# Attention and experts on one core: three buffers for the transposed tokens, loads one step further ahead, another order at the start

## The chip, the cores and the metric

The kernel runs on 1 core of a Trainium2 chip. The metric is the device time of one execution in microseconds; the time before is the median of 3 runs. The profile is of one further execution. TensorE (PE) multiplies matrices, VectorE (DVE), ScalarE (ACT) and GpSimd (POOL) work element by element, SyncE (SP) only issues transfers.

## The reference

The input is x, 8 batches of 512 tokens with 256 features, f32. What is computed, cut to what matters:

```python
xn = layernorm(x)
# attention: 16 heads of 64
q, k, v = split(xn @ qkv_w.T)
q, k = rope(q), rope(k)
scores = q @ k.T / 8 + (-p * log1p(a * abs(i - j)))   # p, a: one number per head
attn = softmax(scores) @ v
# experts: 16 of them, each token goes to its best one, at most 256 tokens each
gate = softmax(xn @ Wg); e = argmax(gate)
y = relu(xn_e @ w1[e]) @ w2[e] * gate[e]     # 0 for tokens beyond an expert's 256
out = x + attn @ out_w.T + y
```

## The kernel before

**Steps and stages.** The 16 heads are cut into 4 groups of 4. One step s is one group g = s // 8 with one batch b = s % 8, so there are 32 steps. A step has four stages dd = 0 to 3; d = 4 s + dd counts them through. A stage projects one of the four products that the next step needs (`project_qk(s + 1, pair, part)`: q or k of a pair of heads, 128 x 512), computes the scores of two units (`score`; a unit is one pair of heads and 128 queries, for which PE makes two 128 x 512 products, VectorE adds the bias and takes the row's bound, ScalarE takes exp), transposes the units of the stage before in 32 x 32 blocks on VectorE (`turn`), and, in every second stage, hands a pair's transposed scores to `move`. Attention times v (`attend`) follows five stages after; `project_out` for step s - 2 is in stage 0, `project_v` in stages 0 and 1.

**Queues.** The order on each engine is the order in which the program calls (`tc.manual_schedule()`): every engine works through its own list, and waits are on data and on buffers. SyncE's list holds nearly all transfers. `move` issues 16 transfers pt<-z of 128 KB, one rd<-turned and two rb<-rd (the reciprocal row sums, through HBM). Beside them stand the running sums y (`load_y`, `store_y`, 512 KB), the expert weights w, and xnT<-xnd.

**Transposed tokens.** `normalise(b)` makes the normalised tokens xn on ScalarE. `transpose_normed(b)` transposes them on PE, and ScalarE copies the result to the tile xnT (128 x 2 x 512). The first four batches use the pool `xpool` for it, with 2 buffers; the xnT of a batch is kept in HBM (xnd[b]) for the later groups. These stores, and those of xn (xrd), are put in the list `stores` and taken from it in later stages by POOL. From step 4 on, `load_normed(s)` loads the tile again: SyncE issues it at the end of stage 1 of step s - 2. With two buffers, the tile takes the place of that of step s - 2, whose last reader is `project_v(s - 2, 1)` in the same stage.

**The start.** Ahead of the loop, batch 0 is normalised and transposed, and the four products of step 0 are made: q and k of pair 0, then, after 14 matmuls whose result is not used (`keep_warm(14)`) and the scores of two units, q and k of pair 1. Each product is turned by its position (rope): VectorE swaps halves (`stream_shuffle` into sh), then three passes multiply by cos, by sin and add (`turn_by`). POOL makes the passes for all later products; at the start VectorE makes those of k of both pairs and of half of q of pair 0. `bias_tables` stage 1 scales the tables of the score bias on POOL.

**The middle and the end.** Up to step 3 the stages also hold the layer norm of the later batches and their logits (`moments`, `deviations`, `logits`), from stage 16 on the routing of the tokens to the experts (`route`, one piece a stage, on VectorE for the most part), and then the experts (`expert_work`), spread over the stages up to the last five steps. The experts' results are gathered and added in those last steps. The last step transposes its scores on PE (`turn_last`).

`product` makes each product of 128 output rows as two products of 64 rows, side by side in the array. It is line 200 of the profile for all projections and all products of the experts. PSUM pools: ps_sc (4 banks), ps_av (1), ps_mm (2), ps_po (1).

Of the kernel before, what the change touches and what calls it, by code (L numbers as in the profile page):

```python
# [19 lines left out]
P = 128  # L20
# [17 lines left out]
def attention_and_experts(  # L38
# [22 lines left out]
    rope = ctx.enter_context(tc.tile_pool(name="rope", bufs=2))  # L61
    xpool = ctx.enter_context(tc.tile_pool(name="xpool", bufs=2))
    ypool = ctx.enter_context(tc.tile_pool(name="ypool", bufs=2))
# [131 lines left out]

    def product(o, w, v, start, stop):

        for c in range(2):
            half = slice(c * D, (c + 1) * D)
            nc.tensor.matmul(o[half], w[:, half], v, start=start, stop=stop)  # L200


    mv = const.tile([P, NT, 2], F32, name="mv")
    rstd = const.tile([P, NT], F32, name="rstd")
    off = const.tile([P, NT], F32, name="off")

# [35 lines left out]

    def load_normed(s):
        xnT = xpool.tile([P, 2, S], F32, tag="xnT", name=f"xnT_{s}")
        nc.sync.dma_start(xnT, xnd[s % B])
        xnTs[s] = xnT
# [19 lines left out]
    def transpose_normed(b, copies=None):  # L266
        xn = xns.pop(b)
        if b < 4:
            xnT = xpool.tile([P, 2, S], F32, tag="xnT", name=f"xnT_{b}")
            xnTs[b] = xnT  # L270
        else:
            xnT = early.tile([P, 2, S], F32, tag="xt", name=f"xnT_{b}", bufs=2)
        for mc in range(2):
            pool, tag = ((ps_av, "av"), (ps_mm, "mm") if b == 2 else (ps_po, "po"))[mc]
            pt = pool.tile([P, S], F32, tag=tag, name=f"xt_{b}_{mc}")
            for i in range(TB):
                nc.tensor.transpose(
                    pt[:, i * P : (i + 1) * P], xn[:, i, mc * P : (mc + 1) * P], ident
                )
            (copies or (nc.scalar.copy,) * 2)[mc](xnT[:, mc, :], pt)  # L280
        stores.append(lambda: nc.gpsimd.dma_start(xnd[b], xnT))
        xns[b] = xnT
# [12 lines left out]
    def logits(b):  # L295

        xnT = xns.pop(b)
        pl = ps_po.tile([P, P], F32, tag="po", name=f"lgp_{b}")
        for mc in range(2):
            for i in range(TB):  # L300
                nc.tensor.matmul(
                    pl[i * 32 : (i + 1) * 32, :], wg[:, mc, :], xnT[:, mc, i * P : (i + 1) * P],
                    start=(mc == 0), stop=(mc == 1),
                )
        lgT[b] = early.tile([P, P], F32, tag="lgT", name=f"lgT_{b}")
        nc.scalar.copy(lgT[b], pl)
# [14 lines left out]
    def route():  # L321
# [30 lines left out]
        )  # L352
        slot = rp.tile([P, CAP], F32, name="slot")
        nc.gpsimd.iota(
# [31 lines left out]
        nc.vector.tensor_reduce(top, oh, AX.X, ALU.max)  # L386
        oh16 = rp.tile([P, NT, E], BF16, name="oh16")
        nc.vector.tensor_tensor(oh16, oh, spread(top), ALU.is_equal)
# [187 lines left out]

    def project_qk(s, pair, part, turn_too=True):
        g, b = divmod(s, B)
        wq, _ = weights[g]
        ps = ps_mm.tile([P, S], F32, tag="mm", name=f"qk_{s}_{pair}_{part}")  # L580
        c0 = part * GC + pair * P
        for mc in range(2):
            product(
                ps, wq[:, mc, c0 : c0 + P], xnTs[s][:, mc, :], start=(mc == 0), stop=(mc == 1),
            )
        sh = rope.tile([P, S], F32, tag="sh", name=f"sh_{s}_{pair}_{part}", bufs=3)
        nc.vector.stream_shuffle(sh, ps, ROT)  # L587
        t = qkpool.tile([P, S], F32, tag=f"qk{part}{pair}", name=f"t_{s}_{pair}_{part}")
        qk[s, pair, part] = t
        if not turn_too:  # L590
            return ps, sh, t
        nc.scalar.copy(t, ps)  # L592
        turn_by(nc.gpsimd, t, t, sh, slice(0, S))
# [6 lines left out]
    def project_v(s, i2):  # L600
        g, b = divmod(s, B)
        wq, _ = weights[g]
        if i2 == 0:
            vals[s] = qkpool.tile([P, TB, GC], F32, tag="v", name=f"v_{s}")
        pool, tag = ((ps_av, "av"), (ps_mm, "mm"))[i2]
        ps = pool.tile([P, 2, GC], F32, tag=tag, name=f"v_{s}_{i2}")
        for i in range(2):
            c0 = (2 * i2 + i) * P
            for mc in range(2):
                product(  # L610
                    ps[:, i, :], xnTs[s][:, mc, c0 : c0 + P], wq[:, mc, 2 * GC :],
                    start=(mc == 0), stop=(mc == 1),
                )
        nc.scalar.copy(vals[s][:, 2 * i2 : 2 * i2 + 2, :], ps)
# [166 lines left out]

    def project_out(s, i2, o=None):
        o = o or oTs
        _, wot = weights[s // B]
        ps = ps_mm.tile([P, 2, DM], F32, tag="mm", name=f"po_{s}_{i2}")
        for i in range(2):
            c0 = (2 * i2 + i) * P
            for pair in range(2):
                product(
                    ps[:, i, :], o[pair][:, c0 : c0 + P], wot[:, pair, :],  # L790
                    start=(pair == 0), stop=(pair == 1),
                )
# [62 lines left out]
    keep_warm(8)  # L855
    rotation(1)
    nc.vector.tensor_scalar_max(ab[:, 1, :], ab[:, 1, :], 0.01)
    bias_tables(0, 0, 1)
    moments(1, (0,))
    transpose_normed(0, (nc.vector.tensor_copy, nc.vector.tensor_copy))  # L860
    moments(1, (1,))
    deviations(1, 2, nc.gpsimd)
    q0 = project_qk(0, 0, 0, False)
    k0 = project_qk(0, 0, 1, False)
    nc.scalar.copy(q0[2][:, 2 * P :], q0[0][:, 2 * P :])
    normalise(1)
    turn_by(nc.vector, q0[2], q0[0], q0[1], slice(0, 2 * P))
    turn_by(nc.vector, k0[2], k0[0], k0[1], slice(0, S))
    keep_warm(14)
    score(*units[0])  # L870
    score(*units[1])
    turn_by(nc.gpsimd, q0[2], q0[2], q0[1], slice(2 * P, S))
    bias_tables(0, 1, 1)
    project_qk(0, 1, 0)
    transpose_normed(1)
    k1 = project_qk(0, 1, 1, False)
    turn_by(nc.vector, k1[2], k1[0], k1[1], slice(0, S))

# [8 lines left out]
    for d in range(duos - TB):  # L887
        s, dd = divmod(d, TB)
        g, b = divmod(s, B)
        pair, half = divmod(dd, 2)  # L890
        project_qk(s + 1, *divmod(dd, 2))
        if s == steps - 2 and dd == 2:
# [3 lines left out]
            for mc in range(2):  # L896
# [3 lines left out]
                )  # L900
        if d in turned_at:
            transpose_normed(turned_at[d])
        score(*units[2 * d + 2])
# [12 lines left out]
        if d in (8, 10):  # L916
            load_x(d // 2 + 2, nc.gpsimd)
        if d == 0:
            stores[1:3] = reversed(stores[1:3])
        for _ in range(min(len(stores), 1 if d < 2 else 3)):  # L920
# [16 lines left out]
        turn(*units[2 * d + 1])  # L937
        if dd == 1 and 4 <= s + 2 < steps:
            load_normed(s + 2)
        if half:  # L940
            move(s, pair)
        if dd == 0 and s > 1:
            project_out(s - 2, 1)
            later.append(lambda s=s: store_y(s - 2, s - 2 >= steps - B + 2))


# [81 lines left out]
    for i2 in range(2):  # L1028
        project_out(s - 2, i2)
    store_y(s - 2, True)  # L1030
# [28 lines left out]
    for i2 in range(2):  # L1059
        project_out(s - 1, i2)  # L1060
    store_y(s - 1, True)
# [58 lines left out]
```

## Time and profile before

| | us |
|---|---|
| median of 3 runs | 1254.71 (1249.23 to 1255.84) |
| the profiled execution | 1253.45 |
| its span | 1251.7 |
| PE busy | 1212.5 (97%) |
| VectorE busy | 889.6 (71%) |
| ScalarE busy | 613.3 (49%) |
| POOL busy | 617.6 (49%) |
| granted clock, mean | 0.992 |
| moved by DMA | 262.10 MB, mean 209 GB/s |

Busy shares are means over parts with different limits. A row of a timeline has start, duration, engine, line, operation, output<-input, shapes and, in brackets, how long the engine was idle before it and what ended that. PE's matmuls count two records each in f32[...]. A row of waits has total, times and the longest.

### The profile page before, as it was taken

How to read it: one execution, taken by the hardware profiler on the slowest of the kernel's cores; microseconds unless marked ns; L12 is line 12 of the kernel's file. 1: busy time of each engine (PE TensorE's matmuls, PEld its weight loads, DVE VectorE, ACT ScalarE, POOL GpSimd, SP SyncE). 2: the span in 40 equal slices, each digit the busy share in tenths (PEclk: the TensorE clock that was granted, in tenths of full speed). 3: DMA queues.
4: the chain of work that ended last, by engine and by line, in shares of the span. 5: the costliest groups of instructions: out<-in, count | busy, mean ns of one | idle time of the engine just before them, and what ended most of it. 6: DMA issues, size and time to landing. Idle time of an engine off the chain costs nothing.

```text
span 1251.7 us, 22571 instructions
## 1 busy us (share of the span) xinstructions
PE 1212.5 (97%) x7694; PEld 559.8 (45%) x7694; DVE 889.6 (71%) x2255; ACT 613.3 (49%) x1429; POOL 617.6 (49%) x614
## 2 busy tenths in 40 slices
PE   8799999999999999999999999999999999999998
PEld 5234433333344444444444454545444544433344
DVE  6988899999875666656556666666666656688763
ACT  6565654466453443444544344444455444356562
POOL 4776754455543443443534344444445433299770
PEclk9899999999999999999999999999999999999999
DMA  4488998888798896867877778977777787689883
GB/s 136 140 221 234 271 239 211 205 202 204 189 246 224 243 248 172 244 182 201 211 212 198 224 196 227 240 212 212 215 181 209 195 233 193 158 223 237 242 236 109
DMA packets 150978, 262.10 MB, mean 209 GB/s; under 512 B 31744, under 2 KB 95504, under 8 KB 150864
## 3 DMA queue, kind: packets, MB, share of 16 engines
q1 hardware_dynamic: 143392, 238.61, 71.4%
q0 software_dynamic: 6368, 20.99, 5.9%
q8 instruction: 61, 1.00, 0.4%
q10 hardware_dynamic: 1104, 1.07, 0.2%
q14 instruction: 53, 0.43, 0.1%
HBM read 99.12 MB, written 31.42 MB: 104 GB/s over the span
## 4 chain that ended last, share of the span: by engine, by line
PE 80%; DMA 8%; SPq 4%; DVE 3%; ACT 2%; issue 1%; POOL 1%; ACTq 0%; DVEq 0%
PE po L200 18%; PE sc L635 16%; PE qk L200 15%; PE av L749 14%; PE v L200 8%; PE ph L200 7%; DMA xnT<-xnd 3%; SPq L672 3%; DMA pt<-z 2%; DMA w<-in_w 2%; ACT xn L255 1%; DVE z L646 1%; PE xdp L510 1%; ACT z L650 1%; PE zt L695 1%
## 5 line engine op out<-in xcount | busy, mean ns | idle before, releaser
L596 POOL TENSOR_TENSOR t<-t,cos_t 128x512 f32<-128x512 f32 (+1 forms) x126 | 161.4, 1281 | 529.0 <-ACT t L592 527.9
L650 ACT ACTIVATE z<-z,st 128x512 f32<-128x512 f32 x512 | 363.3, 711 | 36.7 <-DVE st L646 30.2
L646 DVE CUSTOM_DVE_ANT_1 z<-sc,kb 128x512 f32<-128x512 f32 x512 | 322.5, 686 | 27.3 <-PE sc L635 23.9
L659 DVE STREAM_TRANSPOSE z<-z 128x512 f32<-128x512 f32 x496 | 314.7, 682 | 0.0
L200 PE MATMUL qk<-xnT,wq 128*64 128x512 f32 x1024 | 245.4, 600 | 13.4 <-DMA xnT<-xnd 8.7
L635 PE MATMUL sc<-t,t 64*128 64x512 f32 x1024 | 257.2, 621 | 0.6 <-DVE t L598 0.6
L592 ACT COPY t<-qk 128x512 f32<-128x512 f32 x125 | 73.0, 584 | 342.2 <-DVE sh L587 340.2
L749 PE MATMUL av<-pt,v 128*64 128x512 f32 x992 | 228.6, 603 | 0.6 <-DMA rb<-rd 0.5
L587 DVE LOAD_MASK_SELECT sh<-qk x128 | 1.8, 14 | 243.1 <-PE qk L200 238.4
L598 POOL TENSOR_TENSOR t<-t,sh 128x512 f32<-128x512 f32 (+1 forms) x126 | 160.7, 1276 | 9.9
L597 POOL TENSOR_TENSOR sh<-sh,sin_t 128x512 f32<-128x512 f32 (+1 forms) x126 | 161.3, 1280 | 0.0
L635 PEld LDWEIGHTS sc<-t,t 64*128 64x128 f32 x1024 | 89.1, 188 | 161.4 <-issue 133.3
L749 PEld LDWEIGHTS av<-pt,v 128*64 128x64 f32 x992 | 66.7, 137 | 150.4 <-issue 130.3
L200 PEld LDWEIGHTS qk<-xnT,wq 128*64 128x64 f32 x1024 | 71.2, 137 | 118.5 <-issue 83.1
L200 PE MATMUL po<-wo,o 128*64 128x256 f32 x1024 | 122.5, 382 | 0.0
L200 PE MATMUL po<-w,hT 128*64 128x256 f32 x1024 | 118.4, 380 | 1.4 <-DMA w<-in_w 1.2
L200 PE MATMUL v<-wq,xnT 128*64 128x256 f32 x992 | 117.8, 380 | 0.0
L200 PE MATMUL ph<-xdT,w 128*64 128x256 f32 x1024 | 117.5, 380 | 0.0
L650 ACT ACTIVATION_READ_ACCUMULATOR z<-z,st 128x1 f32 x512 | 95.8, 187 | 0.0
L587 DVE STREAM_SHUFFLE sh<-qk 128x512 f32<-128x512 f32 x128 | 93.8, 733 | 0.7
L200 PEld LDWEIGHTS po<-wo,o 128*64 128x64 f32 x1024 | 70.8, 137 | 52.1 <-ACT t L592 8.3
L200 PEld LDWEIGHTS po<-w,hT 128*64 128x64 f32 x1024 | 72.5, 137 | 47.8 <-issue 7.4
(154 smaller groups left out, 807.6 us busy)
## 6 DMA issues: line engine op xcount, KB each, us to landing
pt<-z SPq DMA_DIRECT2D x992, 128.0 KB
w<-in_w SPq DMA_DIRECT2D x64, 512.0 KB
rb<-rd SPq DMA_DIRECT2D x124, 128.0 KB
xnT<-xnd SPq DMA_DIRECT2D x28, 512.0 KB
yd<-y SPq DMA_DIRECT2D x26, 512.0 KB
y<-yd SPq DMA_DIRECT2D x24, 512.0 KB
xrd<-xn POOLq DMA_DIRECT2D x8, 512.0 KB
xnd<-xnT POOLq DMA_DIRECT2D x8, 512.0 KB, 7.9
```

The source lines that it names most:

```text
L200: nc.tensor.matmul(o[half], w[:, half], v, start=start, stop=stop)
L587: nc.vector.stream_shuffle(sh, ps, ROT)
L592: nc.scalar.copy(t, ps)
L596: eng.tensor_tensor(t[:, c], ps[:, c], cos_t[:, c], ALU.mult)
L597: eng.tensor_tensor(sh[:, c], sh[:, c], sin_t[:, c], ALU.mult)
L598: eng.tensor_tensor(t[:, c], t[:, c], sh[:, c], ALU.add)
L635: nc.tensor.matmul(sc[j].rearrange("p (g c k) -> p g c k", g=TB, k=32), q[r, qc * P : (qc + 1) * P], k[r, :].rearrange("p (c g k) -> p g c ...
L646: nc.vector.tensor_tensor_reduce(z, sc[j].rearrange("p (g c k) -> p g c k", g=TB, k=32), bias, -0.125, 3.0e38, ALU.add, ALU.min, st[:, j : ...
L650: nc.scalar.activation(z, z, AF.Exp, bias=st[:, j : j + 1], scale=-1.0, accum_out=sums[s, pair][:, j, qc : qc + 1],)
L659: nc.vector.transpose(z, z)
L672: nc.sync.dma_start(pt[g * 32 : (g + 1) * 32, qi].rearrange("p c j q -> p (c j q)"), z[qi * 32 : (qi + 1) * 32, g].rearrange("p c j q k -> ...
L749: nc.tensor.matmul(av[j * D : (j + 1) * D, :].rearrange("p (a q) -> p a q", q=P), vals[s][:, kc, c0 : c0 + D], pts[s, pair][:, :, kc, j, : ...
```

## The change

- `xpool` has 3 buffers instead of 2. `load_normed` takes the queue as an argument. For batches 4 to 7 of the first group SyncE loads as before, two steps ahead in stage 1; from step 8 on it loads three steps ahead, in stage 2, right behind `load_y`.
- The stores of batches 0 and 1 to xnd are issued by SyncE at once, not by POOL from the list; the line that swapped two entries of the list goes.
- `project_qk` is cut into `qk_product` (PE) and `partners` (VectorE's shuffle). At the start all four products of step 0 are made ahead of the scores, two of them in score banks, and the 14 unused matmuls go. ScalarE copies q and k of pair 1, POOL makes their three passes in the order q first half, k, q second half; VectorE only shuffles them. The scaling of pair 1's bias tables stands earlier on POOL, and an Exp on one column stands ahead on ScalarE.
- In stages 0 and 1 of the loop the projection of the next step stands behind the scores and v. In stages that transpose a batch, the transposes stand between the product and its shuffle.
- In the last step, v and the output products of steps 29 and 30 are made in full shape (`wide`).
- Smaller tiles move: mv, rstd and off lie in the pool `early`, oh16 in a token buffer, and slot (the numbers 0 to 255 against which positions are compared) is bf16. The logits of batch 2 use the bank ps_av.

```diff
-    xpool = ctx.enter_context(tc.tile_pool(name="xpool", bufs=2))
+    xpool = ctx.enter_context(tc.tile_pool(name="xpool", bufs=3))
...
-    def product(o, w, v, start, stop):
-
-        for c in range(2):
-            half = slice(c * D, (c + 1) * D)
+    def product(o, w, v, start, stop, wide=False):
+
+        for c in range(1 if wide else 2):
+            half = slice(0, P) if wide else slice(c * D, (c + 1) * D)
             nc.tensor.matmul(o[half], w[:, half], v, start=start, stop=stop)
...
-        stores.append(lambda: nc.gpsimd.dma_start(xnd[b], xnT))
+        if b < 2:
+            nc.sync.dma_start(xnd[b], xnT)
+        else:
+            stores.append(lambda: nc.gpsimd.dma_start(xnd[b], xnT))
...
-        pl = ps_po.tile([P, P], F32, tag="po", name=f"lgp_{b}")
+        pool, tag = (ps_av, "av") if b == 2 else (ps_po, "po")
+        pl = pool.tile([P, P], F32, tag=tag, name=f"lgp_{b}")
...
-        slot = rp.tile([P, CAP], F32, name="slot")
+        slot = rp.tile([P, CAP], BF16, name="slot")
...
+    def project_qk(s, pair, part, between=None):
+        ps = qk_product(s, pair, part)
+        if between is not None:
+            transpose_normed(between)
+        sh, t = partners(s, pair, part, ps), qk[s, pair, part]
         nc.scalar.copy(t, ps)
         turn_by(nc.gpsimd, t, t, sh, slice(0, S))
...
+    nc.scalar.activation(early.tile([P, 1], F32, name="unused"), quarter, AF.Exp)
     nc.vector.tensor_scalar_max(ab[:, 1, :], ab[:, 1, :], 0.01)
     bias_tables(0, 0, 1)
+    bias_tables(0, 1, 1)
...
-    q0 = project_qk(0, 0, 0, False)
-    k0 = project_qk(0, 0, 1, False)
-    nc.scalar.copy(q0[2][:, 2 * P :], q0[0][:, 2 * P :])
+    half0, half1, whole = slice(0, 2 * P), slice(2 * P, S), slice(0, S)
+    pk0 = qk_product(0, 0, 1)
+    pq0 = qk_product(0, 0, 0)
+    pq1 = qk_product(0, 1, 0, ps_sc, "sc")
+    pk1 = qk_product(0, 1, 1, ps_sc, "sc")
+    sk0 = partners(0, 0, 1, pk0)
+    sq0 = partners(0, 0, 0, pq0)
+    q0, k0, q1, k1 = qk[0, 0, 0], qk[0, 0, 1], qk[0, 1, 0], qk[0, 1, 1]
+    nc.scalar.copy(q0[:, half1], pq0[:, half1])
+    nc.scalar.copy(q1, pq1)
+    nc.scalar.copy(k1, pk1)
     normalise(1)
-    turn_by(nc.vector, q0[2], q0[0], q0[1], slice(0, 2 * P))
-    turn_by(nc.vector, k0[2], k0[0], k0[1], slice(0, S))
-    keep_warm(14)
+    turn_by(nc.vector, q0, pq0, sq0, half0)
+    turn_by(nc.vector, k0, pk0, sk0, whole)
+    sq1 = partners(0, 1, 0, pq1)
+    sk1 = partners(0, 1, 1, pk1)
     score(*units[0])
     score(*units[1])
-    turn_by(nc.gpsimd, q0[2], q0[2], q0[1], slice(2 * P, S))
-    bias_tables(0, 1, 1)
-    project_qk(0, 1, 0)
+    turn_by(nc.gpsimd, q0, q0, sq0, half1)
+    turn_by(nc.gpsimd, q1, q1, sq1, half0)
+    turn_by(nc.gpsimd, k1, k1, sk1, whole)
+    turn_by(nc.gpsimd, q1, q1, sq1, half1)
     transpose_normed(1)
-    k1 = project_qk(0, 1, 1, False)
-    turn_by(nc.vector, k1[2], k1[0], k1[1], slice(0, S))
...
-        project_qk(s + 1, *divmod(dd, 2))
+        if d > 1:
+            project_qk(s + 1, *divmod(dd, 2), between=turned_at.get(d))
...
-        if d in turned_at:
-            transpose_normed(turned_at[d])
...
-        if d == 0:
-            stores[1:3] = reversed(stores[1:3])
...
-        if dd == 1 and 4 <= s + 2 < steps:
-            load_normed(s + 2)
+        if dd == 1 and 4 <= s + 2 < B:
+            load_normed(s + 2, nc.sync)
+        if dd == 2 and B <= s + 3 < steps:
+            load_normed(s + 3, nc.sync)
...
+        if d < 2:
+            project_qk(s + 1, *divmod(dd, 2))
...
-        project_out(s - 2, i2)
+        project_out(s - 2, i2, wide=True)
...
-        project_out(s - 1, i2)
+        project_out(s - 1, i2, wide=True)
```

## The prediction

> **What bounds the kernel now.** I read the page's busy rows and slices first, then the table by stage, then the waits (PE's and SyncE's own), then the chain of waits and the timeline at the places that these name.
>
> ```profile
> PE 1212.5 (97%) x7694; PEld 559.8 (45%) x7694; DVE 889.6 (71%) x2255; ACT 613.3 (49%) x1429; POOL 617.6 (49%) x614
> ...
> PEclk9899999999999999999999999999999999999999
> ```
>
> ```profile
> 163.00:350.00 187.00, 178.42 (x1030) 71.25 (x1026) 176.30 (x455) 100.47 (x237) 100.07 (x86) 1.00 0.83 207
> ...
> 400.00:1124.00 724.00, 722.62 (x4800) 347.12 (x4796) 462.09 (x1126) 328.06 (x757) 311.25 (x257) 1.00 0.78 210
> ```
>
> Columns: stretch, length, busy PE, PEld, DVE, ACT, POOL, clock, DMA share, GB/s. From 400 to 1124 us TensorE is busy 722.6 of 724 us at full clock: that stretch only shifts, whatever happens ahead of it. All that can be won is TensorE's idle time before 400 and after 1124. It lies at few places:
>
> ```profile
> PE qk L200 <- DMA xnT<-xnd: 8.7, 6, 2.7
> PE lgp L301 <- ACT xnT L280: 6.6, 1, 6.6
> ```
>
> ```profile
> 54.73 1.15 POOL L281 DMA_DIRECT2D xnd<-xnT  x2
> ...
> 59.07 1.07 ACT L280 COPY xnT<-xt 128x512 f32<-128x512 f32 x2 [3.05 <-DMA xnd<-xnT]
> ...
> 59.71 1.14 PE L301 MATMUL lgp<-xnT,wg 128*32 128x128 f32 x16 [6.61 <-ACT xnT L280]
> ...
> 64.59 0.01 DVE L587 LOAD_MASK_SELECT sh<-qk  x1 [2.10 <-POOL nt L233]
> ```
>
> Batch 2's tokens wait for one of two xnT buffers until POOL's late store of batch 0 has landed; PE stands 6.6 us and the clock drops (second digit of PEclk). And this is VectorE in the start, which before 66 us is the fuller engine where PE isn't stalled:
>
> ```profile
> 29.99 0.01 DVE L587 LOAD_MASK_SELECT sh<-qk  x1 [2.21 <-PE qk L200]
> ...
> 31.24 1.16 DVE L597 TENSOR_TENSOR sh<-sh,sin_t 128x512 f32<-128x512 f32 x1
> ...
> 32.43 1.64 DVE L598 TENSOR_TENSOR t<-t,sh 128x512 f32<-128x512 f32 x1
> ```
>
> From 66 to 390 us a third queue matters, SyncE's:
>
> ```profile
> 214.63 0.36 SPq L245 DMA_DIRECT2D xnT<-xnd  x1
> 215.09 2.85 SPq L672 DMA_DIRECT2D pt<-z  x4
> 218.04 0.53 SPq L677 DMA_DIRECT2D rd<-turned  x1
> 218.61 10.26 SPq L672 DMA_DIRECT2D pt<-z  x12
> 228.91 1.30 SPq L680 DMA_DIRECT2D rb<-rd  x2
> 230.26 0.60 SPq L772 DMA_DIRECT2D y<-in_x  x1
> ```
>
> It issues without a pause: one step (two pairs) takes it 30.9 us (214.63 to 245.54), while PE's groups of a step sum to 29.5 (four qk of 1.94, four duos of scores of 1.92, two av of 3.58, v and po of 3.45 each). The xnT load sits in this queue behind two moves, so PE waits for it; in the timeline av starts only 2 to 5 us after the rb issue that it needs has ended (230.2 and 235.05 here).
>
> **The change part by part.** The sum is made against the profiled execution: 1253.45 us, span 1251.7; it lies 1.3 under the median of 1254.71.
>
> *A. Start.* Products for q0, k0, q1, k1 run from 15.6 to 23.1 us in place of two products and 14 idle matmuls (3.39 us from 19.17), so the scores still begin at 23.1, when k0 is turned (23.07). VectorE: two shuffles (2 x 0.74) end at 24.5, score passes of units 0 and 1 (4 x 0.61) at 27.0. Copies of q1 and k1 (0.58 each) now precede ScalarE's normalising of batch 1, which ends at 25.9 instead of 24.54; the Exp table load (1.28 at 24.55) has moved ahead of that, so the exponentials still start at 25.9. The transposes of batch 1 end near 26.8 and the next scores reach VectorE near 28.2: a new wait of 1.2. Then 2.45 of score passes, 2.48 of transposes, 0.74 shuffle, 2.8 of moments: the passes of stage 1 start at 36.6, against 42.82 now. Gain 6.2: k1's three passes (3.4) and the 2.21 wait leave VectorE. They go to POOL: q0's half ends at 25.1 as now, then q1's first half (2.2), k1 (3 x 1.28), ready at 31.2, needed at about 34. The second pair's tables (2.10) lie ahead of POOL's deviations, which begin at 17.70 anyway: nothing.
> Stages 0 and 1 now project behind their scores. Two shuffles then fall together and the second product waits for v's copy to free its bank: 1.7 is given back.
>
> *B. Third buffer and SyncE's two stores.* Batch 2 finds a free buffer: the 3.05 / 6.61 us wait goes and with it the slow clock. But VectorE had lost only 2.10 there and 0.64 before its next pass at 65.97; by its work it reaches stage 4 at 58.9 against 65.97. A and B: 6.2 - 1.7 + 2.7 = 7.2. Each store costs its issuer 0.56 us, on SyncE, which has nothing to do before 47.90. The Trainium skill ("DMA: Bandwidth & Descriptors", "Issuing engines are not separate DMA queues") speaks against a gain: the engine that issues changes nothing about the transfer and saves issue time only. By that rule the two stores are worth POOL's 1.15 us. The row at 54.73 shows more: POOL's queue reaches them 38 us after the tokens were ready, beside the first move, whose 12 pt issues take 12.18 us (8.66 at 203.87). I take the row, and use it only to let SyncE keep the 7.2.
>
> The 14 idle matmuls kept the clock up. "TensorE: Matmul & The Clock Gate" (Part 1) halves the clock after an idle window of about 3.4 us, an estimate of 1.7 us of loss. The row that bears on it: the 6.61 us gap did bring the slow slice. In the changed start I find no gap over 1.5 us before 45, because two products of 1.9 fill the place: nothing.
>
> *C. Loads a step further ahead.* From batch 8 on xnT is loaded in stage 2 of step s for s + 3; steps 6 and 7 keep the old distance. PE's waits there are 0.52 and 0.95 (kept), then 1.6, 2.55, 1.6, 1.35: 7.1 could go. SyncE does the same issues though, and one load more in that stretch (0.4 plus a stall of about 2, as now after each load). SyncE starts 5.6 earlier at its first move and more at the second; what PE can win beyond that is the 2 to 5 us between rb and av. I take 3, between 0 and 7.1. The 99 us that SyncE waits for v (L245, nearly all after 400) go too and are worth nothing: there av comes over 20 us after its rb (642.2 and 667.9). What is late next before 350 us is rb.
>
> *D. Tail.* The last loads move from 1123.8 and 1159.3 to before 1110.
>
> ```profile
> 1166.54 2.50 PE L200 MATMUL qk<-xnT,wq 128*64 128x512 f32 x8 [2.70 <-DMA xnT<-xnd]
> ...
> 1168.96 3.08 PE L635 MATMUL sc<-t,t 64*128 64x512 f32 x8
> ...
> 1194.21 3.65 PE L749 MATMUL av<-pt,v 128*64 128x512 f32 x16 [0.47 <-DMA rb<-rd]
> ```
>
> PE wins 2.7 and the 1.65 by which the next two groups are slow: 4.4. At 1194 it meets rb, last of an unbroken SyncE queue; that loses two loads and about 1 us of stall, 2 to 5 in all. I take 4.0.
>
> *E. Full-shape products.* Two half-width passes start 7 ns apart and take 0.216 us for 256 columns; the full-width idle matmuls take 0.112 for 128: the same. A change of tile shape costs about 0.1; one goes (po to zt). 0.1.
>
> *F. The rest.* The bf16 slot may shorten 32 passes of 0.35 on VectorE (0 to 2 us, where SyncE is the limit: 0). Logits of batch 2 in another bank, oh16 in a token buffer, the earlier ScalarE copies of xnT, mv and its kin in another pool: order only, hidden under VectorE and SyncE; 0, at most 1 either way.
>
> Sum: 7.2 + 3.0 + 4.0 + 0.1 = 14.3; 1253.45 - 14.3 = 1239.2, given as 1239.5.
>
> **The rivals.** *R1, SyncE is no limit:* all of C and D arrive, 7.2 + 7.1 + 4.4 + 0.1 + 1 for slot: 1233.6. For it: its stalls are partly DMA landings, which shrink when other traffic goes. Against: no pause in its timeline. *R2, VectorE or the DMA engines swallow it:* DVE is busy 176.3 of 187 us from 163 to 350, DMA share 0.94 from 125 to 150. Half of A and B (3.6), nothing of C, 2 of D: 1247.9. *R3, slower:* xnT's load now stands right behind y's, ahead of the same move. Each 512 KB load now stalls SyncE by about 2 us six issues later. If the pair stalls by 7.6 instead of 3.8, the six steps from 205 to 390 lose 23 us; less 3 of slack, 7.2 and 4.0: +8.6, 1262. It decides from 2.4 us a step on. Against it: bytes and issues per step are the same. *R4, it doesn't do what it says:* a buffer or store dependence keeps the waits, and A is lost at stage 4: within 3 us of now.
>
> **How the numbers follow.** Main case 0.60, R1 0.15, R2 0.15, R4 0.05, R3 0.05. A measurement here can tell about 0.5%, 6.3 us (1248.4). The main case and R1 count as faster, of R2 two thirds: 0.85; same 0.10; slower 0.05. The range goes from R1 with a further 3 us (A and B at 8.5, D at 5, runs spread by some us) to just past R2: 1230 to 1249.
>
> **What would show it.** In the changed profile: "PE lgp <- ACT xnT" gone and the second PEclk digit 9; VectorE's first pass of stage 1 near 36.6 and of stage 4 near 59; PE's waits for xnT only before 225 us; rb in PE's or PEld's waits before 350 (main case) or not (R1); at the end no wait near 1150, and an rb wait of up to 2 us near 1180. Wrong if the stretch before PE is full (400 now) shrinks by under 5 or over 16 us.

## The result: 0.2 to 0.7% faster, and the profile after

In the first measurement the changed kernel took 1245.26 us (median of 20 runs, 1235.59 to 1251.3) and the kernel before 1253.6 us (20 runs): a ratio of 0.9934, 95% interval 0.9916 to 0.9952. It was measured twice more, on two chips beside the experiments, and gave 0.9970 (0.9952 to 0.9988) and 0.9979 (0.9965 to 0.9994). Single runs spread over 11 us (before) and 16 us (after) in the first measurement alone. So the change brings 8.3 us in one measurement and 3.7 and 2.6 in the two others (1248.05 x 0.0030, 1247.21 x 0.0021), where 14.3 were forecast.

The page of the changed kernel's profiled execution (1245.77 us, span 1244.1, clock 0.994), its busy row and its clock slices:

```profile
PE 1208.4 (97%) x7618; PEld 558.5 (45%) x7618; DVE 885.8 (71%) x2252; ACT 614.4 (49%) x1431; POOL 621.1 (50%) x618
...
PEclk9899999999999999999999999999999999999999
```

The second slice still reads 8. The table by stage (columns as before: stretch, length, busy PE, PEld, DVE, ACT, POOL, clock, DMA share, GB/s):

```profile
163.00:350.00 187.00, 182.33 (x1068) 74.02 (x1066) 176.97 (x463) 104.04 (x247) 103.82 (x89) 1.00 0.81 209
...
400.00:1124.00 724.00, 717.32 (x4738) 343.56 (x4736) 456.88 (x1115) 324.56 (x751) 310.17 (x256) 1.00 0.78 209
```

TensorE is busy for 3.9 us more in the first of these stretches, and for 5.3 less in the second, which was to be full whatever happened. The list of TensorE's waits says what it stands for now (total, times, longest):

```profile
PE po L200 <- DMA w<-in_w: 4.0, 4, 2.0
PE qk L200 <- ACT v L629: 3.5, 1, 3.5
PE av L764 <- DMA rb<-rd: 3.2, 2, 2.3
PE av L764 <- DMA pt<-z: 3.1, 3, 1.9
```

The waits for xnT and for batch 2's copy are gone. In their place stand the experts' weights w, a copy of v, and the pieces (pt) and reciprocals (rb) of the probabilities. The pieces are late before 350 us, the reciprocals only at 1158.59 and 1189.88 us. The wait for w was 1.2 us before, once.

A yardstick for all runs below: the moment at which VectorE ends the last transposition of a pair of heads (pair 2s + p: step s, pair p), read from each kernel's trace. The table gives the us from the span's start to pair 4, between pairs, and from pair 61 to the end; one profile each. The names in front are those of the experiments.

| kernel | to 4 | 4-12 | 12-18 | 18-24 | 24-30 | 30-36 | 36-54 | 54-61 | rest | span |
|---|---|---|---|---|---|---|---|---|---|---|
| before | 112.8 | 128.0 | 94.3 | 123.1 | 128.2 | 128.8 | 380.0 | 105.1 | 51.4 | 1251.7 |
| after | 109.2 | 128.7 | 90.9 | 121.0 | 128.1 | 133.2 | 381.0 | 103.5 | 48.5 | 1244.1 |
| control | 108.2 | 127.0 | 89.8 | 117.9 | 127.0 | 131.8 | 380.1 | 103.4 | 48.1 | 1233.3 |
| control2 | 108.0 | 127.0 | 89.8 | 118.7 | 126.8 | 132.3 | 380.0 | 102.7 | 48.2 | 1233.5 |
| e8_pool_stores | 108.2 | 127.6 | 91.9 | 119.4 | 127.6 | 132.9 | 380.4 | 106.1 | 47.8 | 1241.9 |
| e5_no_turns | 106.5 | 129.2 | 91.8 | 119.3 | 127.5 | 132.2 | 380.8 | 107.9 | 48.1 | 1243.3 |
| e1_first | 105.7 | 130.7 | 91.0 | 119.8 | 127.6 | 132.1 | 380.1 | 106.0 | 48.1 | 1241.1 |
| e3_behind_move | 108.8 | 128.7 | 89.8 | 118.7 | 134.3 | 131.9 | 382.6 | 107.8 | 48.1 | 1250.7 |
| e13 | 105.5 | 127.5 | 90.2 | 120.2 | 130.9 | 134.2 | 382.6 | 104.3 | 48.1 | 1243.5 |
| only_loads | 111.2 | 127.1 | 91.3 | 122.7 | 127.3 | 133.8 | 380.7 | 103.5 | 48.1 | 1245.7 |
| e2_old_loads | 108.2 | 127.9 | 94.2 | 119.9 | 128.0 | 128.8 | 380.1 | 104.2 | 48.1 | 1239.4 |
| e12 | 105.9 | 128.0 | 94.1 | 120.1 | 127.5 | 129.1 | 380.1 | 102.5 | 48.1 | 1235.4 |
| e17 | 106.0 | 128.3 | 94.6 | 122.5 | 132.0 | 128.9 | 380.1 | 107.1 | 48.1 | 1247.6 |
| e6_split | 105.9 | 128.7 | 89.9 | 119.5 | 127.5 | 129.0 | 380.0 | 106.4 | 48.5 | 1235.4 |

Columns 12-18 and 30-36 each take one of two values, whatever the chip: 90 to 92 or 94 to 95, and 129 or 132 to 134. They are the two halves of the story of the loads. The profile of before was taken in the first measurement; in the later ones that kernel's median was 1247.2 to 1248.1 us, so the columns in which it lost time to a half-speed clock need not be typical of it. These are 18-24, 54-61 and the rest: in each of them one stretch of 3.41 us runs at half speed, at 386, 1168 and 1212 us.

### The profile page after: what moved, and what is told of

It reads as the page before. It is cut to its first block, busy times and chain, and to the rows that moved or that the text cites. A ratio compares the mean times of both kernels' runs of the same rounds, so it can differ in the third digit from the quotient of the medians.

```text
span 1244.1 us, 22395 instructions
## 1 busy us (share of the span) xinstructions
PE 1208.4 (97%) x7618; PEld 558.5 (45%) x7618; DVE 885.8 (71%) x2252; ACT 614.4 (49%) x1431; POOL 621.1 (50%) x618
## 4 chain that ended last, share of the span: by engine, by line
PE 71%; DMA 9%; DVE 9%; SPq 5%; POOL 2%; issue 2%; ACT 2%; DVEq 0%; ACTq 0%; POOLq 0%
PE po L200 16%; PE sc L650 14%; PE av L764 13%; PE qk L200 12%; PE ph L200 8%; PE v L200 6%; SPq L687 4%; DMA pt<-z 4%; DVE z L661 3%; DMA w<-in_w 2%; DVE z L674 2%; DMA xnT<-xnd 1%; PE xdp L515 1%; DMA xnd<-xnT 1%; PE zt L710 1%
## 5 line engine op out<-in xcount | busy, mean ns | idle before, releaser
L661 DVE CUSTOM_DVE_ANT_1 z<-sc,kb 128x512 f32<-128x512 f32 x512 | 322.6, 686 | 28.2 <-PE sc L650 23.9
L200 PE MATMUL po<-wo,o 128*64 128x256 f32 (+1 forms) x992 | 122.7, 383 | 0.3 <-ACT t L607 0.3
L200 PEld LDWEIGHTS po<-wo,o 128*64 128x64 f32 (+1 forms) x992 | 72.1, 139 | 52.1 <-ACT t L607 9.7
## 6 DMA issues: line engine op xcount, KB each, us to landing
pt<-z SPq DMA_DIRECT2D x992, 128.0 KB
rb<-rd SPq DMA_DIRECT2D x124, 128.0 KB
```

The source lines that it names most:

```text
L661: nc.vector.tensor_tensor_reduce(z, sc[j].rearrange("p (g c k) -> p g c k", g=TB, k=32), bias, -0.125, 3.0e38, ALU.add, ALU.min, st[:, j : ...
```

## The experiments

Two places of the changed profile were in question: what ate the start's gain, and what took time out of the middle. Times can be compared directly within a chip: the first four share one, the next four (control to e5_no_turns) another, the last four a third.

**e1_first: stage 1 projects ahead of its scores.**

```diff
-        if d > 1:
+        if d > 0:
             project_qk(s + 1, *divmod(dd, 2), between=turned_at.get(d))
...
-        if d < 2:
+        if d < 1:
             project_qk(s + 1, *divmod(dd, 2))
```

> Stage 1 projects ahead of its score products again, as it did before the change; only stage 0 keeps its projections behind. Theory (the second product of stage 1 has to wait for ScalarE's copy of v, which stands behind the exponentials): the wait of 3.49 us at 43.7 us goes, the half-speed stretch of the clock at 40.5 to 47.4 goes or shrinks, the passes of stage 2 begin near 46 to 48 instead of 49.42, and the end comes 2 to 5 us sooner than the changed kernel, near 1241 to 1243. Rival (VectorE, held beside GpSimd's passes, limits this stretch anyway): the wait goes but stage 2 begins within 1 us of 49.42 and the end within 1 us of 1245. Second rival (the projections ahead hold the scores up as in the prediction's account of the old order): stage 1 begins 1 to 3 us later and the end is 1 to 3 us later.

1243.55 us, ratio 0.9974 (0.9953 to 0.9995). In the changed kernel stage 1 projects behind v, so stage 2's projection comes right behind these two and meets this (TensorE's and ScalarE's timelines):

```profile
43.13 0.56 ACT L629 COPY v<-v 128x512 f32<-128x512 f32 x1
43.74 3.68 PE L200 MATMUL qk<-xnT,wq 128*64 128x512 f32 x8 [3.49 <-ACT v L629]
47.35 2.88 PE L650 MATMUL sc<-t,t 64*128 64x512 f32 x8
```

The product needs one of the two banks of ps_mm. Stage 1's projection lies in one and v in the other, and v's copy is behind four exponentials on ScalarE. TensorE stands 3.49 us, then runs eight matmuls in 3.68 us that take 1.94 at full clock, and VectorE's passes of stage 2 wait for the scores. In e1_first, the same product and scores:

```profile
40.76 1.94 PE L200 MATMUL qk<-xnT,wq 128*64 128x512 f32 x8 [0.56 <-ACT t L607]
42.63 1.99 PE L650 MATMUL sc<-t,t 64*128 64x512 f32 x8
```

A wait of 0.56 us in place of 3.49, and full clock. Stage 2's passes begin at 45.94 us, not 49.42, stage 4's at 60.22, not 63.72, and pair 4 is turned at 105.7, where the unchanged order has 108.0 to 109.2. The theory holds for the place. About the end the times alone say less: e13 below differs from e3_behind_move by this edit only and is 2.8 us faster on the same chip, with overlapping intervals.

How much of this is the wait and how much the clock, e5_no_turns below lets one estimate: it has the same wait, at full clock all along, and its stage 2 begins at 46.99 us (it leaves out some of GpSimd's passes). So the wait alone costs about 1 us (46.99 against 45.94). One half-speed stretch of 3.41 us behind it brings 48.2 to 48.5 (the controls, e2_old_loads, e8_pool_stores), two bring 49.1 to 49.4 (the first profile, e3_behind_move).

**e3_behind_move: the load one stage earlier, behind the pieces.**

```diff
-        if dd == 2 and B <= s + 3 < steps:
-            load_normed(s + 3, nc.sync)
         if half:
             move(s, pair)
+        if dd == 1 and B <= s + 3 < steps:
+            load_normed(s + 3, nc.sync)
```

> The load of transposed tokens three batches ahead is issued one stage earlier, behind the pieces of the probabilities, so that it no longer stands directly ahead of the experts' weights on SyncE's queue. Theory (the loads' new place makes the weight loads land late between 400 and 1124): PE's waits for w fall from 4.0 us in 4 to about the 1.2 to 1.4 of before, the half-speed stretch at 600 goes, and the end comes 3 to 6 us sooner, near 1240. Rival (the waits for w are chance, or come from all of SyncE's list, not from its order): waits for w stay over 3 us and the time within 1.5 us of 1245. Other rival (the load is now ahead of the rows of inverse sums of a later pair): waits for rb grow and the time is 1 to 4 us more.

1251.28 us, ratio 1.0030 (1.0011 to 1.0050): slower, against the theory, and the waits for w grew to 7.7 us. SyncE's timeline shows where the load came to stand:

```profile
587.04 4.63 SPq L687 DMA_DIRECT2D pt<-z  x6
591.72 1.30 SPq L695 DMA_DIRECT2D rb<-rd  x2
593.12 0.55 SPq L245 DMA_DIRECT2D xnT<-xnd  x1
593.71 0.43 SPq L787 DMA_DIRECT2D y<-yd  x1
594.24 0.38 SPq L553 DMA_DIRECT2D eo<-eot  x1
594.72 1.96 SPq L495 DMA_DIRECT2D w<-in_w  x2
```

One stage earlier in the program is not earlier in time: the pieces take SyncE until the next stage, and behind them the load is in the same burst, still ahead of the weights. The edit did not test what it was meant to.

**e13: both edits.** The edit is the sum of the two diffs.

> Both edits together: stage 1 projects ahead of its scores, and the load three batches ahead stands behind the pieces of the probabilities. If both theories hold the gains add, less what SyncE's queue gives back before 350 us: 1237 to 1240. If only one holds, the time is that of the one; if neither, 1245 within 1.5 us.

1248.47 us, ratio 1.0011 (0.9991 to 1.0032). Only the start's half holds: pair 4 at 105.5, waits of PE's po for w 9.4 us.

**e2_old_loads: three buffers, loads at their old place.**

```diff
-        if dd == 1 and 4 <= s + 2 < B:
+        if dd == 1 and 4 <= s + 2 < steps:
             load_normed(s + 2, nc.sync)
-        if dd == 2 and B <= s + 3 < steps:
-            load_normed(s + 3, nc.sync)
```

> Three buffers as in the changed kernel, but the loads at their old place and two batches ahead, behind which a wait for the buffer was the rule. Theory (the further loads gain about 3 to 4 us before 350 and 4 to 5 at the end, and give back up to 6 in the middle through the weights): the waits of PE for w return to 1.2 to 1.4 us, waits for xnT before 350 us and at the end return in part, and the time is 0 to 4 us more than the changed kernel, 1245 to 1249. Rival (the third buffer alone takes the wait away, since its old user is a batch further back): no wait for xnT, the weights in time, and the end 3 to 6 us sooner than the changed kernel, near 1240. Rival (the order of loads carries the whole gain): 1250 or more.

1244.34 us, ratio 0.9968 (0.9952 to 0.9985), about the changed kernel's own 0.9970 and 0.9979. What moved is inside. First the changed kernel's SyncE ahead of its longest wait for w, then TensorE's row with that wait, then SyncE in e2_old_loads:

```profile
582.78 7.24 SPq L687 DMA_DIRECT2D pt<-z  x9
590.07 1.29 SPq L695 DMA_DIRECT2D rb<-rd  x2
591.40 0.60 SPq L787 DMA_DIRECT2D y<-yd  x1
592.10 0.38 SPq L245 DMA_DIRECT2D xnT<-xnd  x1
592.57 0.38 SPq L553 DMA_DIRECT2D eo<-eot  x1
593.04 1.72 SPq L495 DMA_DIRECT2D w<-in_w  x2
```

```profile
600.91 2.51 PE L200 MATMUL po<-w,hT 128*64 128x256 f32 x16 [1.99 <-DMA w<-in_w]
```

```profile
571.89 0.43 SPq L245 DMA_DIRECT2D xnT<-xnd  x1
578.19 2.47 SPq L687 DMA_DIRECT2D pt<-z  x4
...
591.45 0.61 SPq L787 DMA_DIRECT2D y<-yd  x1
592.15 0.38 SPq L553 DMA_DIRECT2D eo<-eot  x1
592.63 1.12 SPq L495 DMA_DIRECT2D w<-in_w  x2
```

At the old place the load of 512 KB goes out at 571.89, and then SyncE waits 5.8 us for VectorE's turns anyway: the load has a gap to itself. At the new place it is the second of five large transfers, whose last is issued at 593.97 and wanted at 598.92 (600.91 less the wait), and the weights land 1.99 us late. Pairs 30 to 36 take 128.8 us here; over all runs they take 128.8 to 129.1 in the five kernels that issue the load ahead of the pieces by then, and 131.8 to 134.2 in the nine that issue it behind them. Waits for w are 1.5 us, but the waits for xnT before 350 us are back (5.0 us in four), and pairs 12 to 18 take 94.2 instead of 90 to 92.

**control: the changed kernel again.**

> The changed kernel as it is, beside the variants. Its ratio to the kernel before was 0.9934 in the first measurement. If a chip differs little in what the change meets, 0.992 to 0.995 again; if part of the gain hangs on how soon a transfer lands on the chip at hand, 0.996 or above. Either way a second profile should show waits of PE for w of 3 to 6 us, the wait of 3.5 us for the copy of v at 43.7, and a step of 131 to 134 us from pair 30 to pair 36, as the first profile did.

1244.16 us, ratio 0.9970 (0.9952 to 0.9988). The wait for v's copy came back to 0.01 us, waits for w were 3.5 us. Its profiled execution (1235.08 us) is the fastest of its 18, so its row in the table shows a good run, not the usual one.

**e17: both halves, with the load three steps ahead at the old place.**

```diff
-        if dd == 2 and B <= s + 3 < steps:
+        if dd == 1 and B <= s + 3 < steps:
             load_normed(s + 3, nc.sync)
```

(with e1_first's edit)

> Stage 1 projects ahead of its scores, and the load three batches ahead is issued in stage 1 ahead of the pieces of the probabilities (while SyncE has to wait for the turns of that stage anyway). Theory (the weights come late because SyncE issues the load of tokens in the burst behind the pieces; where it stands ahead of the pieces it costs nothing): waits for w at 1.5 us, pairs 30 to 36 in 128.8 us, pairs 12 to 18 in 91 us as with the further loads, waits for v's copy gone; 6 to 9 us faster than the control. Rival (loading three batches ahead itself takes the transfers' time from the weights): waits for w over 4 us and no more than 3 us faster than the control.

1243.77 us, ratio 0.9974 (0.9956 to 0.9993): no faster than the control. Two of its numbers are worth more than its time. Pairs 12 to 18 took 94.6 us although every load was three steps ahead, and pairs 30 to 36 took 128.9. So neither column follows the distance; both follow the place. With the load ahead of the pieces SyncE is the tighter limit: from 233 to 340 us each av starts 0.4 to 2.1 us after the last issue of rb ahead of it has ended, in control 1.8 to 7.8 us after it, and in e17 TensorE waits for pt there (3.6 us from 233 to 330 us; control has no such wait above 0.3). Why the order costs SyncE time is open: from 233 to 330 us it waited 6.0 us for y and 5.2 for xnT in e17, 2.7 and 4.9 in control, but over 163 to 350 us the first profile and that of before hardly differ in the wait for y (8.5 and 9.0). Here the first experts' weights were late as well, by 3.13 us at 418 and 2.95 at 515, in the two columns that are longer than e12's (18-24 and 24-30). Why they were late stays open, and with it whether the distance costs something there.

**e12: stage 1 as in e1_first, loads as in e2_old_loads.** The edit is the sum of those diffs.

> Stage 1 projects ahead of its scores, and the loads are two batches ahead at their old place, with three buffers. Theory: the gain of the first edit (2 to 3 us) and of the loads at the old place add: 4 to 7 us faster than the control, pairs 12 to 18 in 94 us as before the change, so 1 to 3 us slower than the version that also loads three ahead. Rival (what the start gains is swallowed before 225 us): within 1 us of the kernel with the old loads alone, ratio to before near 0.997.

1241.70 us, ratio 0.9956 (0.9941 to 0.9971), 2.5 us faster than the control beside it; the intervals overlap. Columns to 4 and 30-36 have the better values, 12-18 the worse (94.1).

**e5_no_turns: the start without GpSimd's passes over q and k of pair 1 of step 0.**

```diff
-    turn_by(nc.gpsimd, q1, q1, sq1, half0)
-    turn_by(nc.gpsimd, k1, k1, sk1, whole)
-    turn_by(nc.gpsimd, q1, q1, sq1, half1)
```

> One look at the start: the changed kernel without GpSimd's turns of the second pair's query and key of the first batch, nine passes of some 1.3 us in all three groups; that part of the rotation is left out. Theory (VectorE is held while GpSimd's passes run): the VectorE passes of 1.10 and 1.12 us near 37 and 38.5 us take 0.17 to 0.2 us again and the passes of stage 1 begin near 37 instead of 39.58. Rival (VectorE's own list is the limit there): stage 1 begins within 0.5 us of 39.58.

One run, 1245.06 us. Stage 1 begins at 39.79, so the theory's 37 did not come, but the experiment had the wrong passes. In the changed kernel the two long rows on VectorE end with the GpSimd passes that turn the next step's projection, not with those of the start (39.58 is stage 1):

```profile
37.00 1.27 POOL L612 TENSOR_TENSOR sh<-sh,sin_t 128x512 f32<-128x512 f32 x1
38.35 1.28 POOL L613 TENSOR_TENSOR t<-t,sh 128x512 f32<-128x512 f32 x1
...
37.20 1.10 DVE L217 TENSOR_SCALAR ve<-mv 128x4 f32<-128x4 f32 x1
38.54 1.12 DVE L222 TENSOR_SCALAR rstd<-nt 128x4 int32<-128x4 int32 x1
39.58 0.68 DVE L661 CUSTOM_DVE_ANT_1 z<-sc,kb 128x512 f32<-128x512 f32 x1
```

Those were left in, and in e5_no_turns the same pair of rows stands 0.22 us later (37.42 for 1.10, 38.76 for 1.12). That the passes hold VectorE fits both profiles and is not shown by this one.

**only_loads: the kernel before with the third buffer and the loads' new places.** The diff is the change's own, without the start, the stores, the wide products and the other bank for batch 2's logits. The smaller tiles that make room for the buffer are moved as in the change (not shown):

```diff
-    xpool = ctx.enter_context(tc.tile_pool(name="xpool", bufs=2))
+    xpool = ctx.enter_context(tc.tile_pool(name="xpool", bufs=3))
...
-        if dd == 1 and 4 <= s + 2 < steps:
-            load_normed(s + 2)
+        if dd == 1 and 4 <= s + 2 < B:
+            load_normed(s + 2)
+        if dd == 2 and B <= s + 3 < steps:
+            load_normed(s + 3)
```

> The kernel before with the third buffer, the room made for it and the new places of the loads alone: the start, the first stores and the products at the end are as before the change. Theory (of the gain, the loads bring 3 to 4 us from pair 12 to 18, 2 to 4 us around the first experts and 2 at the end, and give back 3 to 6 us in the middle): pairs 12 to 18 in 90 to 91 us, pairs 30 to 36 in 131 to 134 us, and 2 to 4 us faster than before, a ratio of 0.997 to 0.9985. Rival (the prediction's own sum for the loads, with nothing given back): 7 us faster, 0.9945. Second rival (the start carries everything): 0.999 to 1.002.

1247.61 us, ratio 1.0011 (0.9997 to 1.0025). The loads by themselves are worth nothing, against both the 2 to 4 us of the theory and the 7 of the prediction's sum. The columns are as the theory had them: 91.3 and 133.8. By its profile this kernel is 6 us ahead of the one of before; by the times it is not. The profile of before is therefore a poor base for the end and the first experts, as said above.

This kernel also separates two causes that the change takes away together. ScalarE no longer waits for a buffer with batch 2's tokens, and yet TensorE stands at the same place, almost as long, and the clock is at half speed from 56.6 to 63.4 us. First only_loads, then the changed kernel:

```profile
58.13 0.18 DVE L311 COPY lg<-lg 128x64 f32<-128x64 f32 x1
58.46 1.08 PE L301 MATMUL lgp<-xnT,wg 128*32 128x128 f32 x16 [6.18 <-DVE lg L311]
```

```profile
55.81 0.65 PE L305 MATMUL lgp<-xnT,wg 128*32 128x128 f32 x16
59.62 0.18 DVE L315 COPY lg<-lg 128x64 f32<-128x64 f32 x1
```

The logits of batch 2 need the bank ps_po, in which the logits of batch 1 lie until VectorE copies them. In the changed kernel they have another bank, ps_av, and start 3.8 us before that copy does. In before this wait hid behind the buffer's: the copy ended at 59.14, TensorE went on at 59.71. The bank was not tried by itself; that it is needed is read from these rows.

**e8_pool_stores: the first stores by GpSimd again.**

```diff
-        if b < 2:
-            nc.sync.dma_start(xnd[b], xnT)
-        else:
-            stores.append(lambda: nc.gpsimd.dma_start(xnd[b], xnT))
+        stores.append(lambda: nc.gpsimd.dma_start(xnd[b], xnT))
```

> The changed kernel with its first two stores on GpSimd's queue again, one in each of the first stages. Theory (the third buffer alone takes the wait for the stores away; the queue they go by is worth nothing): no wait of ScalarE for a store above 0.5 us, pair 4 turned within 1 us of the changed kernel's 109.2 and 108.2, the time within 1.5 us of the control. Rival (as the prediction had it, part of the gain is SyncE's early store): a wait for a buffer or a late first load, pair 4 turned 1 to 3 us later.

1244.90 us, ratio 0.9978 (0.9963 to 0.9992), beside control2's 0.9979. Pair 4 at 108.2 and 108.0, and no wait of ScalarE for a store. The queue is worth nothing in the changed kernel.

**control2: the changed kernel a third time.**

> The changed kernel once more as it is, so that the variants have a third comparison. With 0.9934 and 0.997 measured before: 0.9935 to 0.997. Its profile should again have pairs 12 to 18 in 90 to 91 us, pairs 30 to 36 in 131 to 134 us, and the wait of 3.5 us for the copy of v.

1244.32 us, ratio 0.9979 (0.9965 to 0.9994), 89.8 and 132.3 us in the two columns. Its profiled execution (1235.19 us), too, is its fastest.

**e6_split: each place where it is the better one.**

```diff
-        if dd == 2 and B <= s + 3 < steps:
+        if dd == 2 and B <= s + 3 <= B + 4:
             load_normed(s + 3, nc.sync)
+        if dd == 1 and B + 5 <= s + 2 < steps:
+            load_normed(s + 2, nc.sync)
```

(with e1_first's edit)

> Stage 1 projects ahead of its scores; the loads for batches 8 to 12 stand behind the pieces, three batches ahead, as in the changed kernel; from batch 13 on they stand ahead of the pieces again, two batches ahead, as before the change. Theory (behind the pieces is the better place while the pieces are what comes late, ahead of them once the experts' weights are): pairs 12 to 18 in 90 to 91 us and pairs 30 to 36 in 128.8 us in one profile, waits of PE for w under 2 us after 450 us, and 4 to 7 us faster than the control, a ratio to before of 0.992 to 0.994. Rival (the two places only exchange waits, and what one saves comes back at the end): no faster than the version with old loads and the early projection, 0.9956.

1238.17 us (6 runs, 1236.82 to 1240.8), ratio 0.9932 (0.9919 to 0.9946). The changed kernel beside it on the same chip has 0.9979 with an interval that doesn't reach it; the medians are 6.2 us apart. Its TensorE waits:

```profile
PE av L764 <- DMA rb<-rd: 3.6, 1, 3.6
...
PE po L200 <- DMA w<-in_w: 1.1, 3, 0.7
```

Pairs 12 to 18 take 89.9 us and pairs 30 to 36 129.0, the better value of both columns, and pair 4 is turned at 105.9. It beats both the kernel before and the changed one. Against e12, measured on another chip (0.9956, 0.9941 to 0.9971), the intervals still touch, and the two profiles have the same span: what e6_split saves in 12-18 (94.1 to 89.9) it loses in 54-61 (102.5 to 106.4). So the rival, that the two places only exchange waits, is not excluded. What is left late is rb at the end (3.64 us near 1180 us), which the prediction had as the next limit there.

## Why the prediction was right or wrong

*The sign and the size.* Faster was right; 14.3 us was too much. The range held because the half-swallowed case was in it: 1245.26 lies nearer to that rival's 1247.9 than to 1239.5, though for other reasons than it gave (VectorE, the DMA engines). The later 3.7 and 2.6 us lie under even that rival's 5.6, so that the range held is in part luck. The loads' part of the sum, 7 us, is worth nothing by only_loads, and e2_old_loads, which has all but their new place, gains as much as the changed kernel.

*A, the start.* Stage 1 gained 3.2 us (42.82 to 39.58), not 6.2. The sum took VectorE's small passes at the 0.17 us of before; two took 1.10 and 1.12 beside GpSimd's passes. That is 1.9 of the 3.0 missing. Most of the rest is earlier: the sum let both shuffles of pair 1 end at 24.5, but in the changed kernel the second waits for GpSimd's last pass over q of pair 0, which the sum itself put at 25.1, and the next scores reach VectorE at 29.47, not 28.2:

```profile
25.45 0.01 DVE L599 LOAD_MASK_SELECT sh<-qk  x1 [1.46 <-POOL t L613]
```

*A's "1.7 is given back" and the clock.* This step failed most plainly, in the clock and not in the wait. The prediction named the mechanism, the product that waits for v's copy, and 1.7 us for it is not too little: at full clock the wait of 3.49 us costs about 1 (e5_no_turns). But the wait brought half speed with it: over 40.5 to 47.4 us the granted clock was 0.64, and stage 2 began 3.5 us later than without it (49.42 to 45.94). The prediction weighed the Trainium skill's clock gate page ("TensorE: Matmul & The Clock Gate", Part 1) only against the removed idle matmuls, found "no gap over 1.5 us before 45", and set the clock to nothing. The gap over 1.5 us was the stall that it had itself put there. With the stall taken out (e1_first) pair 4 comes 7.1 us sooner than before (112.8 to 105.7); with it 3.6 in the first profile and 4.6 and 4.8 in the controls. That 7.1 looks like the 7.2 of A and B is luck: the 7.2 already has the 1.7 taken off, and without that the sum says 8.9.

*B, the third buffer and the queue.* The waits of 3.05 and 6.61 us are gone, as said, but not by the buffer alone. only_loads has the buffer, and TensorE still stands 6.18 us, for the bank. The other bank, which the prediction put under F at 0, so has a share in B's 2.7. That SyncE's queue keeps the gain is refuted: e8_pool_stores is the same in time and at pair 4. The Trainium skill's rule ("DMA: Bandwidth & Descriptors", "Issuing engines are not separate DMA queues") was right here, and the row at 54.73 us that was set against it was a lateness which the changed kernel no longer feels.

*C, the loads.* The 3.0 us before 350 measured 3.4 (94.3 to 90.9), and SyncE's queue remains late in some profiles: in the first TensorE waits 3.1 us for pt there. The sign that was named, rb in the waits before 350 us, did not show. The reason given, a load further ahead, was not the reason: e17 has the distance and not the gain. The place behind the pieces has it.

*"That stretch only shifts."* This is the step that cost the loads' part its value. From 400 to 1124 us TensorE was full in the profile of before and was taken as closed. The new place put 512 KB ahead of the experts' weights, which had been just in time (1.2 us late, once). Pairs 30 to 36 went from 128.8 to 133.2 us. The two waits for w in them (1.99 and 0.87 us) and the half-speed stretch behind the first, an estimated 1.7 us (half of 3.41), account for these 4.4 (their sum is 4.6). A stretch that is full has transfers that are just early enough; a moved transfer passes them.

*D, the end.* From pair 54 on the profiles show 4.5 us (156.5 to 152.0), 4.0 were forecast. That they agree is luck as well. What D named, the load of xnT near 1166 us and the rb behind it, lies in column 54-61, which is 1.6 us shorter: the wait for xnT is gone, and rb waits of 0.85 and 2.31 took most of its place. The other 2.9 lie in the last column, where TensorE waited 2.32 us at 1211 in the profile of before (0.29 in the changed one) and the clock was at half speed behind it. Nor was the loads' move needed: e2_old_loads, with the third buffer and the old place, has no wait for xnT at the end. How much the usual run gains there stays open; only_loads, at no gain in time, has the same columns.

*E and F.* only_loads has the narrow products and the same last column (48.1) as the controls: 0.1 us or less, as said. Of F the bank counts, as under B; its other items were not tried by themselves.

*The slower rival* (the pair of loads doubling SyncE's stalls) didn't come: from 163 to 350 us SyncE waited 10.8 us for xnT and 8.5 for y, 12.6 and 9.0 before. Its place was wrong, its idea nearly right: the load that moved did delay what was behind it, but after 400 us and in another transfer.

## What to carry to other kernels

Ask of a moved transfer what now stands behind it in its queue at each phase of the kernel, not only where it was late: one place was worth 3 to 4 us while the pieces were late and cost 3 to 5 once the weights were. Place a load by time, ahead of a wait in which the queue would idle, rather than by how many steps ahead it is. And a stall that the sum accepts must be followed to the engine that stands and to its clock.

## What the runs showed of the hardware

- The same idle time of TensorE had different prices. The wait for v's copy was 3.48 to 3.50 us in seven kernels; the eight matmuls behind it took 1.94 us in e5_no_turns (clock 1.00 over 40.5 to 47.4), 3.03 in control (0.79), and 3.68 in the first profile (0.64). The traces show how. In each of them the clock changes only on a grid of 3.41 us, which lies elsewhere in every run, and half speed follows a window of this grid in which TensorE was idle for some 2 us. The windows of 3.41 us, with the clock (0.50 is half speed), first in the first profile, then in e5_no_turns (columns: stretch, length, busy PE, clock, DMA share, GB/s):

```profile
38.96:42.37 3.41, 1.29 (x8) 1.00 0.00 0
42.37:45.79 3.42, 2.04 (x6) 0.50 0.19 69
45.79:49.20 3.41, 3.41 (x8) 0.50 0.87 241
49.20:52.61 3.41, 3.41 (x30) 1.00 0.87 192
```

```profile
38.60:42.01 3.41, 1.88 (x10) 1.00 0.01 2
42.01:45.42 3.41, 1.46 (x8) 1.00 0.07 19
```

  The grid cuts the wait into idle parts of 2.12 and 1.37 us in the first and of 1.53 and 1.95 in the second. Counted over the 14 traces from 20 us on, half speed followed all 24 full-speed windows with 2.03 us of idle or more, 2 of the 34 with 1.5 to 2.02, and 3 of the 4895 with less (1.2 us each, where TensorE transposes tokens near 125 us). A window at half speed was followed by another in all 8 cases with 0.7 us of idle or more, and by full speed in all 29 with 0.64 or less. The Trainium skill's clock page ("TensorE: Matmul & The Clock Gate", Part 1) has a freely running window of about 3.4 us, which the grid bears out, but names one idle window as the condition for half speed; here some 60% of one was enough.
- The clock is much of the spread. Over the 69 runs of the kernel before on the first experiments' chip, a straight line through time and mean granted clock falls 1.5 us for each 0.001 (correlation 0.76); on the two other chips 1.0 and 0.8 (0.63 and 0.49). e6_split's six runs have a mean clock of 0.9983, control2's 22 have 0.9951: by these slopes an estimated 2.6 to 4.8 of the 6.2 us between them comes with the clock.
- VectorE's passes of 128 x 4 numbers took 1.10 and 1.12 us instead of 0.17, and each ended within 0.04 us of a GpSimd pass; batch statistics beside another such pass kept their 0.40. The Trainium skill ("SBUF — State Buffer", "SBUF: two separate sides") has a port that the two engines share and that one holds for a whole instruction; that agrees with the two rows. No run here took the GpSimd pass away, so it is not shown as the cause.
